# New planner costs, start slots and first-block slots for a recurrence woven into an MoE kernel

## The chip, the cores and the metric

The kernel runs on one core of one Trainium2 chip. The metric is the device time of one execution in microseconds (us); for the kernel before it is the median of three runs. Beside these there is one profiled execution with its trace. The engines are TensorE (PE in the profile, with its weight loads as PEld), VectorE (DVE), ScalarE (ACT), GpSimd (POOL) and SyncE (SP, which here only issues DMAs).

## The reference

The input `x` is 4 x 1024 tokens of 128 channels. Three layers change it in turn, each behind a layer norm:

```python
x = x + 0.5 * ffn(layernorm(x))
x = x + mamba(layernorm(x))
x = x + 0.5 * ffn(layernorm(x))

# ffn: 8 experts, all of them for every token, hidden width 512
h = silu(x @ w_gate[e]) * (x @ w_up[e]);  out += cw[:, e] * (h @ w_down[e])
# cw: product of two softmaxes over the experts, normalised

# mamba: 256 inner channels, 16 states, convolution over 4 steps
xs, z = split(x @ W_in);  xc = silu(conv4(xs) + conv_b)
dt = softplus((xc @ W_x)[:64] @ W_dt + b_dt);  B, C = the rest of xc @ W_x
h[t] = exp(dt*A) * h[t-1] + dt*xc*B[t]          # for each of 16 states n
y = sum_n h*C + xc*D;  out = (y * silu(z)) @ W_out
```

The recurrence over `t` runs along each of the four sequences.

## The kernel before, in words

The 4096 tokens are cut into 8 blocks of 512 (two blocks to a sequence). There are 16 passes of the ffn, one for each block before the recurrence, `(1, k)`, and one after it, `(2, k)`, in the order (1,0) (1,1) (1,2) (1,3) (2,0) (1,4) (2,1) (1,5) (2,2) (1,6) (1,7) (2,3) ... (2,7). A pass has 8 experts, an expert two **halves**. A half is one product for the gate (`pg`, six matmuls), one for the up branch (`pu`, six matmuls), the SiLU of the gate on ScalarE (`h`, L625), the multiply of both on VectorE (`h`, L657), and the products with the down weights into `pd` (L722; for the experts in `SPL` the operands are split in two parts on ScalarE and VectorE, `hh` L665 and `hl` L667, and go through L697 and L705). `pg` and `pu` have one buffer each: TensorE can't begin the next `pg` before the SiLU of the last has read it, nor the next `pu` before the multiply has read it. A half is counted as four **slots**, and the whole is 256 halves.

Into this stream the mamba layer of each block is woven. Its front (layer norm, `xs` and `z` products, four convolution taps, `xc`, `dbl`, `dt`, softplus, `dx`) is a list of events with a slot each; `START[k]` is the slot of block k that all are counted from, and `FRONT`/`REST` hold the slots of the single steps (`ta`, `xs`, `cv`, `ap`, `xp`, `dp`, `sp`, `df`, `n0`). Then come 16 states n in pairs. A pair is a burst on ScalarE: a table load, four `da` exponentials (L1002), a table load back for the SiLU. Each state then has four steps on VectorE: `prod` (`hb`, L1015), two scans (`hb`, L1021), and `read` (`da`, L1033; in the first block of a sequence also the copy of the last state, L1032). GpSimd adds the result to `y` (L1036). `bcb`, the broadcast of B and C, is loaded by SyncE into three buffers, the next one when a `read` has been issued. The end of a block (`gate`, `outproj`) waits for all 16.

The order on each engine is laid down when the program is built. A planner (`Plan`) keeps one clock for each engine in us, adds a cost for each step that it places, and takes VectorE's steps from two queues: `hi` for short steps (taps, splits, weightings) and `lo` for the recurrence. Before each multiply, `plan.now` fills VectorE with queued steps that would begin earlier than `SL` = 0.3 us before the multiply is ready. So a step's cost decides how many steps are put ahead of the next multiply. The costs in `LOCK` mark the steps that, like GpSimd's, read two operands from SBUF: the planner puts them outside of GpSimd's own steps. An event can have a readiness test: it is held back until the test is met by the planner's TensorE clock, but for no more than `WAIT` (12) slots, after which it is issued and waits on the chip.

ScalarE's bursts are gated by slots as well: `quiet` (softplus) and `turn` (exponentials) let one through only at every eighth slot, and never two in the same slot.

Of the kernel before, what the change touches and what calls it, by code (L numbers as in the profile page):

```python
# [18 lines left out]
BIG = 11  # L19
TMP = 3  # L20
TOL = 0.4
START = (72, 144, 232, 328, 432, 544, 656, 744)
REST = (4, 9, 17, 19, 23, 25, 29, 35, 37)
FRONT = {0: (5, 7, 8, 15, 16, 18, 21, 27, 29)}
ZT = {0: 11}
SOON = (0, 4, 6, 14, 15)
CALM = (4, 5)
# [16 lines left out]
FENDS = {0: 8, 1: 9, 9: 9, 15: 8}  # L44
OUT = 3
SL = 0.3
LOCK = (1.21, 0.71, 1.18, 0.66)
CAP = 5.8
NEVER = 1e9
WAIT = 12  # L50
# [3 lines left out]
class Plan:  # L54
# [74 lines left out]
    def run(self, it):  # L129
# [3 lines left out]
        self.dve = max(self.dve, it[2])  # L133
        if it[1] in LOCK:
            self.dve = self.unlocked(self.dve)
# [5 lines left out]
    def due(self, it):  # L141
        t = max(it[2], self.dve)
        return self.unlocked(t) if it[1] in LOCK else t

# [28 lines left out]
def tile_macaron_mamba_moe(  # L173
# [29 lines left out]
    NBLK = NB * L // TB  # L203
    BPB = L // TB
    FC = F // 128
    ND = DI // 128
# [11 lines left out]
    plan = Plan()  # L218

    def big(name):  # L220
        return sb.tile([P, 2, TB], F32, tag="big", bufs=BIG, name=name)
# [220 lines left out]
    silu_at, h_at = {}, {}  # L442
# [149 lines left out]
    def split(s, e):  # L592
        return s * E + e in SPL
# [34 lines left out]
    def half_products(s, c, i, tag, nm):  # L628
        d = ffn[s]
        e, f = divmod(c, FC)  # L630
        o = ps.tile([P, 2, TB], F32, tag=tag, bufs=1, name=f"{tag}_{nm}")
        cols = [slice((f + q) * P, (f + q + 1) * P) for q in range(2)]
        if (s, c, i) == (0, 0, 0):
            for q in range(2):
                T.matmul(o[:, q, :], wh[e][:, i, cols[q]], d["xh"], start=True, stop=False)
                T.matmul(o[:, q, :], wl[e][:, i, cols[q]], d["xh"], start=False, stop=False)
            for q in range(2):
                T.matmul(o[:, q, :], wh[e][:, i, cols[q]], d["xl"], start=False, stop=True)
            return o
        for q in range(2):  # L640
            T.matmul(o[:, q, :], wh[e][:, i, cols[q]], d["xh"], start=True, stop=False)  # L641
            T.matmul(o[:, q, :], wh[e][:, i, cols[q]], d["xl"], start=False, stop=False)  # L642
            T.matmul(o[:, q, :], wl[e][:, i, cols[q]], d["xh"], start=False, stop=True)  # L643
        return o

    def up_part(s, c):
        d = ffn[s]
        kind, k = order[s]
        e, f = divmod(c, FC)
        nm = f"{kind}_{k}_{c}"  # L650
        g = s * GPS * FC + c
        h = d["hp"]
        pu = half_products(s, c, 1, "pu", nm)
        t = max(silu_at[g], plan.on_pe(1.38, h_at.get(g - 2, 0.0)))

        def mul():
            V.tensor_tensor(h, h, pu, ALU.mult)  # L657

        h_at[g] = d["h_at", c] = d["h_at", c + 1] = plan.now(mul, 1.17, t, SL)
        if split(s, e):  # L660
            hh = sb.tile([P, 2, TB], F32R, tag="big", bufs=BIG, name=f"hh_{nm}")
            hl = sb.tile([P, 2, TB], F32R, tag="big", bufs=BIG, name=f"hl_{nm}")

            def high():
                S.copy(hh, h)  # L665
                d["hl", c] = d["hl", c + 1] = plan.put(
                    lambda: V.tensor_tensor(hl, h, hh.bitcast(F32), ALU.subtract), 1.18, plan.act + 0.1  # L667
                )

            d["hh", c] = d["hh", c + 1] = plan.act_put(high, 1.0, h_at[g], True)  # L670
            d["h", c] = d["h", c + 1] = hh, hl
        else:
            d["h", c] = (h[:, 0, :],)
            d["h", c + 1] = (h[:, 1, :],)
# [151 lines left out]
    riders, slot, burst_at, want = [], [0], [-1], set()  # L826
# [25 lines left out]
    def pool_need(it):  # L852
        if it not in pend:
            plan.need(lambda: it[3])
        while not it[3]:
            pool_one(None)
        return it[4]


    def mamba_events(k):  # L860
        d = {}
# [53 lines left out]
        def conv(i):  # L915
            if i == 0:
                d["cv"] = big(f"cv_{nm}")
            cv, xs = d["cv"], d["xs"]
            assert d["xsp"] > i
            def first_tap():  # L920
                S.activation(
                    cv[:, i, :], xs[:, i, 0:TB], AF.Identity,
                    bias=cb_sb[:, i : i + 1], scale=cw_sb[:, i, 0:1],
                )
                plan.put(lambda: tap(1), 0.71, plan.act + 0.61)

            it = plan.act_put(first_tap, 0.61, 0.0)
            d.setdefault("cv_it", []).append(it)

            def tap(q):  # L930
                V.scalar_tensor_tensor(
                    cv[:, i, :], xs[:, i, q : q + TB], cw_sb[:, i, q : q + 1], cv[:, i, :],
                    ALU.mult, ALU.add,
                )
                if q < 3:
                    plan.put(lambda: tap(q + 1), 0.71)
                else:
                    d["conv"] = d.get("conv", 0) + 1
                    d["cv_at"] = plan.dve + 0.1
# [58 lines left out]
        def exps(n):  # L998
            plan.need_lo(4 * OUT)
            da = d["da", n] = big(f"da_{nm}_{n}")  # L1000
            for i in range(ND):
                S.activation(da[:, i, :], d["dt"][:, i, :], AF.Exp, scale=A_sb[:, i, n : n + 1])  # L1002
            t = plan.on_act(1.22, 0.0, "exp")
            if n == 0:
                if fast:
                    plan.need(lambda: d["dx_it"][3])
                else:
                    t = max(t, pool_need(d["dx_it"]))
            for f, cost in ((prod, 1.21), (lambda n: step(n, 0), 1.2), (lambda n: step(n, 1), 1.2), (read, 1.2)):
                plan.put(lambda f=f: f(n), cost, t, low=True)  # L1010

        def prod(n):
# [5 lines left out]
        def step(n, i):  # L1018
            hb = d["hb"]
            da = d["da", n]  # L1020
            V.tensor_tensor_scan(  # L1021
                hb[:, i, :], da[:, i, :], hb[:, i, :],
                0.0 if first else st_sb[:, i, n : n + 1], ALU.mult, ALU.add,
            )
# [64 lines left out]
        fast = k == 0  # L1089
# [5 lines left out]
        zt = ZT.get(k, 14)  # L1095
        ta, xs, cv, ap, xp, dp, sp, df, n0 = FRONT.get(k, REST)

        def quiet():
            if d.get("dtp") != ND or slot[0] % 8 != 5:
                return False  # L1100
            want.add(k)
            return burst_at[0] < slot[0]
# [5 lines left out]
            (xs, inproj),  # L1108
            (xs, lambda: xsproj(0), lambda: max(free(), d["xlow"][4] if d["xlow"][3] else NEVER)),
            (cv, lambda: conv(0)),  # L1110
            (xs + 2, lambda: xsproj(1), free),
            (cv + 2, lambda: conv(1)),
            (zt, lambda: zproj(0), free),
            (zt + 2, lambda: zproj(1), free),
            (ap + w, act, lambda: d["cv_at"] if d.get("conv") == ND else NEVER),
            (xp + w, xproj, lambda: max(free(), d["xc_at"])),
            (dp + w, lambda: dtproj(0), lambda: max(free(), d["low"][4] if d["low"][3] else NEVER)),
            (dp + w + 2, lambda: dtproj(1), free),
            (sp + w, softplus, lambda: 0.0 if quiet() else NEVER),
            (df + w, dtfin),  # L1120
        ]
        mid = []

        def turn():
            fits = "dx_it" in d and slot[0] % 8 == 5 and burst_at[0] < slot[0]
            return 0.0 if fits and not want and len(plan.lo) <= QUEUE else NEVER

        for q in range(NS // 2):
            def two(q=q):
                burst_at[0] = slot[0]  # L1130
                while riders:
                    riders.pop(0)()
                exps(2 * q)
                exps(2 * q + 1)

            mid += [(n0 + 8 * int(SPR * q) + w, two, turn)]
        back = [
            (EPI + v + GT, gate, lambda: 0.0 if "scanned" in d else NEVER),
            (EPI + v + PO + (0 if quick else POW), outproj, lambda: max(free(), gated_at())),
        ]  # L1140

        def gated_at():
            return (d["gated"][4] if d["gated"][3] else NEVER) if "gated" in d else NEVER
# [5 lines left out]
    def add(base, evs, wait=WAIT):  # L1149
        chains.append([(max(0, base + ev[0]), wait, *ev[1:]) for ev in evs])  # L1150
# [15 lines left out]
    for s in range(len(order)):  # L1166
        add(8 * GPS * s, ffn_events(s))
        kind, k = order[s]
# [4 lines left out]
    for k in range(NBLK):  # L1173
        front, mid, back = mamba_events(k)
        add(START[k], front)
        add(START[k], mid, 99)
        add(START[k], back, 24 if k == NBLK - 1 else WAIT)
    for e in range(1, E):
        add(8 * (e - 1), [(WL, lambda e=e: load_expert(e)), (WS, lambda e=e: split_expert(e))])
    add(8 * E, [(-24, load_mamba)])  # L1180
# [5 lines left out]
    with tc.manual_schedule(engines={ET.PE, ET.Activation, ET.DVE, ET.Pool, ET.SP}):  # L1186
        half = 0
        while chains or done < nst:
            c = 2 * half
# [50 lines left out]
```

## Time and profile before

| | |
|---|---|
| median of three runs (lowest, highest) | 1266.12 us (1266.01, 1266.13) |
| the profiled execution's own time | 1265.99 us |
| its span, first to last instruction | 1264.2 us |
| DVE, ACT, POOL busy | 1138.2, 921.8, 706.1 us |
| granted TensorE clock | 1.0 |
| bytes read from HBM | 109.71 MB, 90 GB/s with the writes |

The profile gives busy time by engine, groups of equal instructions with their mean duration, and for each group the idle time of its engine just before, with what ended it. A record of a matmul lasts longer than the time to the next one, because matmuls are pipelined: in the trace a 128x512 matmul of the gate product lasts 0.40 us and the next one starts 0.23 us later. VectorE's and ScalarE's records overlap a little in the same way.

### The profile page before, as it was taken

The page shows a single profiled execution, that of the slowest core. Times are in us where ns is not written, and L with a number is a line of the kernel's source. Part 1 is how long each engine was busy: PE and PEld are TensorE (multiplying, and loading weights), DVE is VectorE, ACT ScalarE, POOL GpSimd, SP SyncE. Part 2 cuts the span into 40 slices and gives each one's busy share as a digit, 9 for nine tenths or more (in the row PEclk, how much of TensorE's full clock was granted, in tenths as well). Part 3 has the DMA queues.
Part 4 walks back from the last instruction along what each step waited for, and adds up shares of the span by engine and source line. Part 5 has one row for each costly group of instructions (what it writes and reads, how often), then busy time and mean ns, then how long its engine had stood idle before and what let it go on. Part 6 is the DMA issues. An engine that isn't in the chain of part 4 may idle for free.

```text
span 1264.2 us, 14417 instructions
## 1 busy us (share of the span) xinstructions
PE 1245.2 (99%) x4800; PEld 862.0 (68%) x4800; DVE 1138.2 (90%) x1286; ACT 921.8 (73%) x1326; POOL 706.1 (56%) x557
## 2 busy tenths in 40 slices
PE   9999999999999999999999999999999999999998
PEld 7776666666666666666666666666666666668787
DVE  6985699999899999999999999999999999998676
ACT  7684887776777768787788778778777776666653
POOL 1022465757568647775676567757775676554400
PEclk9999999999999999999999999999999999999999
DMA  4501333343343433334343353432433433311011
GB/s 147 158 26 34 107 112 86 101 112 82 81 107 97 118 91 95 93 99 110 99 100 96 92 119 84 120 98 82 113 98 79 110 92 109 103 56 42 26 43 25
DMA packets 75386, 115.09 MB, mean 91 GB/s; under 512 B 7472, under 2 KB 23728, under 8 KB 75312
## 3 DMA queue, kind: packets, MB, share of 16 engines
q1 hardware_dynamic: 75312, 114.19, 33.6%
q8 instruction: 37, 0.61, 0.2%
q14 instruction: 37, 0.30, 0.1%
HBM read 109.71 MB, written 4.46 MB: 90 GB/s over the span
## 4 chain that ended last, share of the span: by engine, by line
PE 70%; DVE 16%; ACT 5%; issue 5%; POOL 3%; DMA 1%; SPq 0%; DVEq 0%; ACTq 0%; POOLq 0%
PE pd L722 19%; PE pu L641 7%; PE pg L641 7%; PE pg L643 7%; PE pu L643 7%; PE pu L642 7%; PE pg L642 7%; DVE hb_m L1021 5%; DVE h L657 4%; PE pd L697 3%; DVE hb_m L1015 2%; DVE da_m L1033 2%; PE pd L705 1%; ACT da_m L1002 1%; ACT h L625 1%
## 5 line engine op out<-in xcount | busy, mean ns | idle before, releaser
L722 PE MATMUL pd<-h,wd 128*128 128x512 f32 x824 | 391.6, 592 | 1.2 <-ACT tmp L735 1.2
L657 DVE TENSOR_TENSOR h<-h,pu 128x1024 f32<-128x1024 f32 x256 | 311.1, 1215 | 76.9 <-PE pu L643 52.5
L1036 POOL TENSOR_TENSOR y_m<-y_m,da_m 128x1024 f32<-128x1024 f32 x128 | 310.5, 2426 | 106.5 <-DVE hb_m L1015 103.2
L625 ACT ACTIVATE h<-pg 128x1024 f32<-128x1024 f32 x256 | 262.7, 1026 | 140.2 <-PE pg L643 135.2
L641 PE MATMUL pg<-xh_f,wh 128*128 128x512 f32 x510 | 266.9, 523 | 0.7 <-ACT h L625 0.7
L744 POOL TENSOR_TENSOR tmp<-tmp,cwb 128x512 f32<-128x512 f32 x98 | 129.1, 1318 | 196.6 <-issue 106.2
L722 PEld LDWEIGHTS pd<-h,wd 128*128 128x128 f32 x824 | 153.5, 188 | 107.9 <-issue 89.6
L641 PE MATMUL pu<-xh_f,wh 128*128 128x512 f32 x512 | 205.8, 402 | 5.8 <-DVE h L657 5.6
L643 PE MATMUL pg<-xh_f,wl 128*128 128x512 f32 x510 | 201.1, 394 | 0.8 <-DVE wl L299 0.8
L643 PE MATMUL pu<-xh_f,wl 128*128 128x512 f32 x512 | 200.5, 392 | 0.0
L642 PE MATMUL pu<-xl_f,wh 128*128 128x512 f32 x512 | 199.9, 391 | 0.0
L642 PE MATMUL pg<-xl_f,wh 128*128 128x512 f32 x510 | 199.4, 391 | 0.0
L1015 DVE TENSOR_TENSOR hb_m<-dx_m,bcb_m 128x1024 f32<-128x1024 f32 x128 | 166.4, 1300 | 1.8
L1021 DVE TENSOR_TENSOR_SCAN hb_m<-da_m,st_sb,hb_m 128x512 f32<-128x512 f32 x128 | 164.2, 1283 | 2.3
L1002 ACT ACTIVATE da_m<-dt_m,A_sb 128x512 f32<-128x512 f32 x256 | 164.0, 711 | 0.6
L1021 DVE TENSOR_TENSOR_SCAN hb_m<-da_m,hb_m 128x512 f32<-128x512 f32 x128 | 156.7, 1224 | 2.6
L1033 DVE TENSOR_TENSOR da_m<-hb_m,bcb_m 128x1024 f32<-128x1024 f32 x128 | 155.8, 1217 | 1.5
L641 PEld LDWEIGHTS pg<-xh_f,wh 128*128 128x128 f32 x510 | 96.0, 188 | 64.8 <-issue 27.4
L747 POOL TENSOR_TENSOR acc<-acc,tmp 128x512 f32<-128x512 f32 x98 | 130.3, 1330 | 7.6
L642 PEld LDWEIGHTS pg<-xl_f,wh 128*128 128x128 f32 x510 | 96.3, 189 | 50.6 <-issue 36.5
L641 PEld LDWEIGHTS pu<-xh_f,wh 128*128 128x128 f32 x512 | 96.1, 188 | 35.4 <-DVE h L657 15.8
L643 PEld LDWEIGHTS pg<-xh_f,wl 128*128 128x128 f32 x510 | 95.6, 187 | 23.2 <-DVE wl L299 1.2
(181 smaller groups left out, 1494.7 us busy)
## 6 DMA issues: line engine op xcount, KB each, us to landing
bcb_m<-bc_m SPq DMA_DIRECT2D x128, 512.0 KB
cwb<-cd_f SPq DMA_DIRECT2D x128, 256.0 KB
out_dram<-x SPq DMA_DIRECT2D x13, 256.0 KB
x<-in_L_attn_x_dram SPq DMA_DIRECT2D x8, 256.0 KB
wraw<-in_L_ffn_w_gate_dram SPq DMA_DIRECT2D x8, 256.0 KB
wraw<-in_L_ffn_w_up_dram SPq DMA_DIRECT2D x8, 256.0 KB
wd<-in_L_ffn_w_down_dram SPq DMA_DIRECT2D x8, 256.0 KB
cd_f<-ct_f SPq DMA_DIRECT2D x64, 4.0 KB
```

Source lines behind the costliest of these rows:

```text
L625: S.activation(h, pg, AF.Silu)
L641: T.matmul(o[:, q, :], wh[e][:, i, cols[q]], d["xh"], start=True, stop=False)
L642: T.matmul(o[:, q, :], wh[e][:, i, cols[q]], d["xl"], start=False, stop=False)
L643: T.matmul(o[:, q, :], wl[e][:, i, cols[q]], d["xh"], start=False, stop=True)
L657: V.tensor_tensor(h, h, pu, ALU.mult)
L722: T.matmul(d["pd"], wd[e][:, cols], h[0], start=(f == 0), stop=(f == FC - 1))
L747: it = put(lambda: G_.tensor_tensor(acc, acc, t, ALU.add), 1.25, at)
L1002: S.activation(da[:, i, :], d["dt"][:, i, :], AF.Exp, scale=A_sb[:, i, n : n + 1])
L1015: mul = V.tensor_tensor(hb, d["dx"], bcb[:, 0:1, :].to_broadcast([P, ND, TB]), ALU.mult)
L1021: V.tensor_tensor_scan(hb[:, i, :], da[:, i, :], hb[:, i, :], 0.0 if first else st_sb[:, i, n : n + 1], ALU.mult, ALU.add,)
L1033: V.tensor_tensor(da, hb, bcb[:, 1:2, :].to_broadcast([P, ND, TB]), ALU.mult)
L1036: it = pool_put(lambda: G.tensor_tensor(d["y"], d["y"], da, ALU.add), 2.4, plan.dve)
```

## The change

No instruction is added or taken away: on each engine both programs hold the same instructions, in another order. The costs that the planner books for the multiply, the taps, `prod` and the first scan are set to other values (and `LOCK` with them, which finds a step by its cost; the weight split of an expert, 1.21, is no longer one of them). Blocks 5, 6 and 7 start 8, 16 and 24 slots sooner. Block 0's front has other slots, its first tap on ScalarE is issued at once instead of being queued, and its softplus and first exponentials may go at every fourth slot. The end of a block may be held back for 40 slots instead of 12 (24 for the last).

```diff
-START = (72, 144, 232, 328, 432, 544, 656, 744)
+START = (72, 144, 232, 328, 432, 536, 640, 720)
 REST = (4, 9, 17, 19, 23, 25, 29, 35, 37)
-FRONT = {0: (5, 7, 8, 15, 16, 18, 21, 27, 29)}
+FRONT = {0: (4, 6, 7, 11, 12, 14, 16, 19, 19)}
...
-LOCK = (1.21, 0.71, 1.18, 0.66)
+LOCK = (1.27, 0.75, 1.18, 0.66)
...
-        h_at[g] = d["h_at", c] = d["h_at", c + 1] = plan.now(mul, 1.17, t, SL)
+        h_at[g] = d["h_at", c] = d["h_at", c + 1] = plan.now(mul, 1.14, t, SL)
...
-                plan.put(lambda: tap(1), 0.71, plan.act + 0.61)
+                plan.put(lambda: tap(1), 0.75, plan.act + 0.61)
 
             it = plan.act_put(first_tap, 0.61, 0.0)
+            if fast:
+                plan.act_run(it)
...
-                    plan.put(lambda: tap(q + 1), 0.71)
+                    plan.put(lambda: tap(q + 1), 0.75)
...
-            for f, cost in ((prod, 1.21), (lambda n: step(n, 0), 1.2), (lambda n: step(n, 1), 1.2), (read, 1.2)):
+            for f, cost in ((prod, 1.27), (lambda n: step(n, 0), 1.25), (lambda n: step(n, 1), 1.2), (read, 1.2)):
...
-            if d.get("dtp") != ND or slot[0] % 8 != 5:
+            if d.get("dtp") != ND or slot[0] % (4 if fast else 8) != (1 if fast else 5):
...
             fits = "dx_it" in d and slot[0] % 8 == 5 and burst_at[0] < slot[0]
+            if fast and ("da", 0) not in d and "dx_it" in d and slot[0] % 4 == 1:
+                fits = True
...
-        add(START[k], back, 24 if k == NBLK - 1 else WAIT)
+        add(START[k], back, 40)
```

`fast` is true for block 0 alone.

## The prediction

> **What bounds the kernel now.** The page comes first: busy time by engine, then the groups (these lines are from the page).
>
> ```profile
> span 1264.2 us, 14417 instructions
> PE 1245.2 (99%) x4800; PEld 862.0 (68%) x4800; DVE 1138.2 (90%) x1286; ACT 921.8 (73%) x1326; POOL 706.1 (56%) x557
> ...
> L657 DVE TENSOR_TENSOR h<-h,pu 128x1024 f32<-128x1024 f32 x256 | 311.1, 1215 | 76.9 <-PE pu L643 52.5
> ...
> L1015 DVE TENSOR_TENSOR hb_m<-dx_m,bcb_m 128x1024 f32<-128x1024 f32 x128 | 166.4, 1300 | 1.8
> ```
>
> TensorE is busy 99% of the span, and the change takes no matmul away. What can be won is only the time in which TensorE waits. So the next view is who TensorE waits for (us in total, times, longest):
>
> ```profile
> PE pu L641 <- DVE h L657: 5.6, 11, 0.9
> PE pd L705 <- DVE hl L667: 1.7, 1, 1.7
> PE pd L722 <- ACT tmp L735: 1.2, 1, 1.2
> ...
> PE lt_f L485 <- DVE xl_f L471: 0.8, 2, 0.6
> PE pg L643 <- DVE wl L299: 0.8, 1, 0.8
> PE pg L641 <- ACT h L625: 0.7, 1, 0.7
> ```
>
> All fifteen rows of this view add up to 15.3 us, of which about 3 belong to the start and the last pass's end. A wait costs a little more than it shows: a matmul's record lasts 0.40 us and the next may start 0.23 after it, so TensorE is stopped 0.17 longer than it counts as idle. The eleven waits for the multiply thus cost 5.6 + 11 x 0.17 = 7.5 us. That is the largest part and the one that the planner's costs govern. The third view is the load by stage (busy us in 64 us: PE, PEld, DVE, ACT, POOL):
>
> ```profile
> 64.00:128.00 64.00, 61.66 (x255) 45.86 (x254) 43.31 (x57) 41.34 (x73) 13.63 (x20) 1.00 0.10 30
> 1024.00:1088.00 64.00, 63.19 (x242) 42.58 (x241) 62.69 (x63) 43.14 (x56) 45.72 (x33) 1.00 0.39 108
> ```
>
> Before the recurrence VectorE has 20 us of 64 to spare, in the middle 1.3. A step too many ahead of a multiply isn't made up for quickly there. The last view is VectorE's timeline around one such wait:
>
> ```profile
> 235.71 1.22 DVE L657 TENSOR_TENSOR h<-h,pu 128x1024 f32<-128x1024 f32 x1 [0.42 <-PE pu L643]
> ...
> 241.91 1.21 DVE L657 TENSOR_TENSOR h<-h,pu 128x1024 f32<-128x1024 f32 x1
> 243.03 1.23 DVE L1015 TENSOR_TENSOR hb_m<-dx_m,bcb_m 128x1024 f32<-128x1024 f32 x1
> 244.29 2.49 DVE L1021 TENSOR_TENSOR_SCAN hb_m<-da_m,hb_m 128x512 f32<-128x512 f32 x2
> ...
> 248.03 1.21 DVE L657 TENSOR_TENSOR h<-h,pu 128x1024 f32<-128x1024 f32 x1
> ```
>
> The multiply takes 1.12 from start to next start (241.91 to 243.03), `prod` before a scan 1.26, the scan pair 2.53 to the copy. From the multiply at 235.71 to the end of the one at 248.03 VectorE needs 13.53 us. TensorE's steps from the end of the `pu` that the first reads to the start of the `pu` that waits for the third are three `pg` (1.37 each), two `pu` (1.37), six down products (0.856), four `v` (0.229) and a transpose: 13.03. The overrun is 0.50; the trace shows a wait of 0.36, which with the 0.17 is 0.53. So static sums of this kind predict the waits.
>
> **The change, part by part.** The sum is made against the profiled execution's 1265.99 us; the median, 1266.12, is 0.13 above. Both programs hold 4290, 1264, 1248, 562 and 389 instructions on PE, DVE, ACT, POOL and SP, ScalarE's with 154 changes of table in both. Only the order counts.
>
> *Planner costs.* A multiply booked at 1.14 is what the trace shows; `prod`, first scan and taps rise by 0.06, 0.05 and 0.04. A state is booked at 4.92 instead of 4.81, where the trace shows 1.26 + 2.53 + 0.08 + 1.13 = 5.00 above. Fewer steps go ahead of a multiply. I made the sum of the example for every multiply and up to 14 multiplies back, with the means of the groups: before, 19 places have an overrun above -0.25 us; after, 13. Added up from that threshold it is 5.06 us before and 3.14 after, 62%. At the example's place the changed order has the last `read` and copy behind the multiply: 12.08 against 13.03, no wait. Of the 7.5 us I take off 38%: **-2.9**. Bounds: nothing, and all of it, -7.5. What hides the rest is the room for a multiply, one down pair and one `pg` less itself (1.71 + 1.37 - 1.13 = 1.95 us); without that cover each state between two multiplies (1.13 + 5.00 against 4.46) would cost 1.67.
>
> *ScalarE's bursts.* The same sum for the SiLU (it must end before the next `pg`): before 2 places above -0.25, which add up to 0.62; after 5, adding up to 1.47. Three are new in kind. In block 0 softplus and the first exponentials now stand in neighbouring halves (overrun -0.03); in pass (1,2) a burst goes at once after `h` (0.02 and 0.09); in pass (1,7) block 5's last exponentials and block 6's softplus are neighbours: SiLU 0.92, load 1.29, two small and four large exponentials 2.7, load 1.29, SiLU 0.92, load 1.29, softplus 1.08, copy 0.49, load 1.29, SiLU 0.92, in all 12.2 against TensorE's 12.0. Before, one overrun of 0.22 became the 0.7 us wait (0.87 with the 0.17); by the same ratio 1.47 becomes 2.0: **+1.1**. Bounds: -0.9 (no such wait) and +3.5 (0.87 at all five places).
>
> The row for these loads: one at 145.42 lasts 1.28 and the SiLU behind it starts at 146.72, 0.02 us after it. [...]
>
> *Block 0's first tap at once.* On ScalarE it now stands between the copy of `xs0` and the copy `tmp` that frees `pd`, for which TensorE waits at 106.98. The row of the tap (L921) has 0.81 us, 0.71 to the next start. The down products, the `xs1` products and the next `pg` are queued behind that wait: **+0.7**. Below zero it can't go; at most 0.8.
>
> *Pass (1,0).* VectorE's order moves `hl` of the third half into a gap of 1.47 us ahead of the multiply at 24.61, and the `hl` that TensorE waits for at 34.17 comes one multiply (1.13) sooner. But from 34.64 to 70.55 VectorE runs with only 1.0 us of idle time, to the expert weight `wl` that TensorE waits for at 70.6. The same steps lie between in both orders, so most comes back there: **-0.4**, between -1.2 and +0.4.
>
> *Block 7 sooner.* The `xl` of the last pass is made two halves earlier, and its logits 1.5, so the wait of 0.6 (L485) at 1171.4 goes: **-0.7**. Next late is the transpose of the weights (L556, 0.5), where the order is as before.
>
> *What moves and costs nothing.* The recurrences of blocks 5 and 6 begin in the same halves as before (152, 176), block 7's two earlier (200 for 202): they start when the block before leaves the queue, not at `START`. Block 0's first `prod` comes 2 halves sooner, the last `read` of all 1.5. SyncE's queue issues block 0's B and C about one half sooner; the first `bcb` issue was at 129.49 and `prod` at 143.12, so 13.6 us shrink to about 9. DMA moved 0.76 MB from 129.4 to 135, more than one `bcb` of 0.5 MB, so it has landed by then. If that failed, `prod` would hold the next multiply and TensorE behind it, up to 2 us. GpSimd's order and load are the same, but its long steps (2.4 us) will meet VectorE elsewhere: `prod` was held to 2.74 us at worst, a tap to 2.86, so one new meeting costs up to 2.1 and one that goes saves as much. I take 0, by the equal number of steps.
>
> Sum: -2.9 + 1.1 + 0.7 - 0.4 - 0.7 = **-2.2**, 1265.99 to 1263.8, and the same against the median within 0.1. I predict 1263.8.
>
> **Rivals.** Bounds for "same" are 0.2%, 2.5 us: 1263.6 to 1268.7, about what a measurement of this kernel can tell from no change.
>
> *All of VectorE's lateness goes.* The two halves' lead of block 0 is kept, and the multiply is never late: -7.5, -0.7, with +0.7 for the tap: 1258.5. For it: 6 of the 11 waits lie at places where the changed order has no overrun above -0.25. Against: three places still overrun by 0.3 to 0.5, and ends of blocks are as full as before.
>
> *The change doesn't do what it says.* Since the late recurrences begin where they did, there is no more room in the middle; tight places only move. The tap and the bursts cost what the planner saves: 1266.0, within 0.5 either way.
>
> *Slower: neighbouring bursts on ScalarE.* In blocks 0 and 6 two bursts follow each other, and SiLU, multiply and `pg` all queue behind the second. If its real length is over the sum by 1.5 us at each of the five places, TensorE waits 7.5 us there instead of the 0.9 of before. The other terms add up to -3.3, so the total is +3.3: 1269.3. It is slower than before from 0.8 us a place, by more than can be doubted from 1.2. Against: nothing stands between a load and its user in the rows.
>
> **How the numbers follow.** Forecast (1262 to 1265.5) 0.45; all lateness gone, or near to it (below 1262) 0.20; nothing (1265.5 to 1268) 0.20; slower, beyond that, 0.15. Of the forecast half lies below 1263.6. Faster by over 0.2% is 0.20 + 0.23 = 0.43; slower than 1268.7 keeps 0.13; within, 0.44. The range leaves out a tenth on each side: 1258.0, just beyond the whole of the lateness, to 1268.9, just short of the ScalarE rival's time.
>
> **What would show it.** In the profile after: TensorE's waits for the multiply fall from 5.6 us to about 3.5 in seven or eight waits; the wait for SiLU rises from 0.7 to about 1.5; the wait for `tmp` near 107 rises from 1.2 to 1.9; `hl` falls to about 0.5 and `wl` rises by nearly as much; L485's 0.6 is gone; the matmul count and ScalarE's loads are the same. I am wrong if the multiply's waits don't fall, or if TensorE waits anywhere more than 3 us for GpSimd or a DMA.

## The result: 1274.19 us, 0.65% slower

| | before | after |
|---|---|---|
| median of 4 runs each (lowest to highest) | 1266.07 us (1265.76 to 1266.13) | 1274.19 us (1273.82 to 1275.47) |
| ratio, 95% interval | | 1.0065, 1.0051 to 1.0079 |
| profiled run: time, span | 1265.99, 1264.2 us | 1274.01, 1272.2 us |

The changed kernel is 8.1 us slower, against a forecast of 2.2 us faster and a range that ended at 1268.9. The page's first lines of the changed kernel:

```profile
span 1272.2 us, 14425 instructions
PE 1249.2 (98%) x4800; PEld 861.1 (68%) x4800; DVE 1136.6 (89%) x1286; ACT 922.1 (72%) x1326; POOL 705.8 (55%) x557
```

VectorE, ScalarE and GpSimd have the busy time of before. TensorE's rises by 4.0 of the 8 us, with the same number of matmuls; the other 4 us are idle time. TensorE's waits in the changed kernel (us in total, times, longest):

```profile
PE pd L705 <- DVE hl L667: 4.6, 3, 2.6
PE pd L722 <- ACT tmp L735: 2.0, 1, 2.0
PE pg L641 <- ACT h L625: 1.9, 4, 0.9
PE pg L643 <- DVE wl L299: 1.3, 2, 0.8
PE pu L641 <- DVE h L657: 1.2, 3, 0.5
PE pg L641 <- DVE wh L298: 1.1, 1, 1.1
...
PE xs_m L890 <- DVE ex_f L506: 1.0, 1, 1.0
```

The wait that the change is about, the multiply (`pu` <- `h`), fell from 5.6 us in 11 waits to 1.2 in 3, further than forecast. But the operand splits, `hl`, `wl` and `wh`, went from 2.5 to 7.0 us, and `tmp`, SiLU and `xs_m` grew by 3. To see where, I took for each half how much later its `pu` starts than in the kernel before. I call this its lag: +0.3 us at half 12, +3.3 at 16, +2.9 at 20, +6.5 at 28, +7.5 at 60, +6.2 at 224, +9.0 at 228, +8.0 at the end. (Half 24, at +7.6, has six more matmuls of the front ahead of it than before, some 1.4 us of work that is only moved; at the halves listed the number is equal.) So three places lose, pass (1,0), block 0's front and halves 224 to 228, and a middle gains.

**Pass (1,0).** VectorE's rows there, changed kernel (start, length, engine, line):

```profile
68.85 1.21 DVE L657 TENSOR_TENSOR h<-h,pu 128x1024 f32<-128x1024 f32 x1
69.98 0.68 DVE L298 CAST wh<-wraw 128x1024 fp32r<-128x1024 f32 x1
70.70 1.23 DVE L299 TENSOR_TENSOR wl<-wraw,wh 128x1024 fp32r<-128x1024 f32 x1
...
74.65 1.22 DVE L657 TENSOR_TENSOR h<-h,pu 128x1024 f32<-128x1024 f32 x1 [2.12 <-PE pu L643]
75.78 1.22 DVE L667 TENSOR_TENSOR hl<-h,hh 128x1024 fp32r<-128x1024 f32 x1
```

And the same place in the kernel before:

```profile
67.60 0.69 DVE L298 CAST wh<-wraw 128x1024 fp32r<-128x1024 f32 x1
68.20 1.21 DVE L657 TENSOR_TENSOR h<-h,pu 128x1024 f32<-128x1024 f32 x1
69.33 1.22 DVE L299 TENSOR_TENSOR wl<-wraw,wh 128x1024 fp32r<-128x1024 f32 x1
...
71.13 1.21 DVE L667 TENSOR_TENSOR hl<-h,hh 128x1024 fp32r<-128x1024 f32 x1
73.30 1.22 DVE L657 TENSOR_TENSOR h<-h,pu 128x1024 f32<-128x1024 f32 x1 [0.95 <-PE pu L643]
```

There the casting of this expert weight (`wh`) stood one multiply sooner, ahead of the multiply at 68.20, and `hl` stood ahead of the next multiply. Now TensorE waits 1.25 us for it at 70.81 and 0.63 for `wl` at 71.98. So its next `pu` is late as well, VectorE idles 2.12 us for it, and the `hl` that could have filled this gap stands behind the multiply: TensorE waits another 1.76 us at 77.06. (The times at a place, here and below, are taken from issue to issue; they are some 0.17 us longer than in the view of the waits.)

**Block 0's front.** On ScalarE the first tap stands ahead of the copy `tmp` that TensorE waits for:

```profile
109.45 0.81 ACT L921 ACTIVATE cv_m<-xs_m,cb_sb,cw_sb 128x512 f32<-128x512 f32 x1
110.17 0.56 ACT L735 COPY tmp<-pd 128x512 f32<-128x512 f32 x1
```

Stretches of 2, 4 and 4 us around this wait and behind it (stretch, length; busy time of PE, PEld, DVE, ACT, POOL; granted clock; DMA):

```profile
110.00:112.00 2.00, 1.21 (x3) 0.73 (x4) 0.75 (x1) 0.74 (x2) 1.18 (x1) 0.94 0.00 0
112.00:116.00 4.00, 4.00 (x10) 2.45 (x10) 1.26 (x2) 1.40 (x2) 1.64 (x3) 0.61 0.31 66
116.00:120.00 4.00, 4.00 (x18) 2.73 (x16) 1.47 (x3) 2.11 (x3) 0.00 (x0) 1.00 0.00 0
```

TensorE waits 2.2 us, up to 110.79, and from 111.75 its granted clock is 0.5 for 3.41 us: 10 matmuls in 4 us instead of 18.

**The end.** VectorE's rows there, changed kernel:

```profile
1137.35 1.22 DVE L1017 TENSOR_TENSOR hb_m<-dx_m,bcb_m 128x1024 f32<-128x1024 f32 x1
1138.61 2.61 DVE L1023 TENSOR_TENSOR_SCAN hb_m<-da_m,st_sb,hb_m 128x512 f32<-128x512 f32 x2
1141.13 1.21 DVE L657 TENSOR_TENSOR h<-h,pu 128x1024 f32<-128x1024 f32 x1
1142.25 1.21 DVE L667 TENSOR_TENSOR hl<-h,hh 128x1024 fp32r<-128x1024 f32 x1
```

The `hl` at 1142.25 stands behind `prod`, two scans and the multiply of a later half. TensorE waits 2.7 us for it, to 1143.52. In the kernel before, the same `hl`, here the first row, stood ahead of that multiply and of the recurrence's steps:

```profile
1131.23 1.21 DVE L667 TENSOR_TENSOR hl<-h,hh 128x1024 fp32r<-128x1024 f32 x1
...
1134.10 1.21 DVE L657 TENSOR_TENSOR h<-h,pu 128x1024 f32<-128x1024 f32 x1
1135.23 1.22 DVE L1015 TENSOR_TENSOR hb_m<-dx_m,bcb_m 128x1024 f32<-128x1024 f32 x1
```

### The profile page after: what moved, and what is told of

It reads as the page before. It is cut to its first block, busy times and chain, and to the rows that moved or that the text cites. A ratio compares the mean times of both kernels' runs of the same rounds, so it can differ in the third digit from the quotient of the medians.

```text
span 1272.2 us, 14425 instructions
## 1 busy us (share of the span) xinstructions
PE 1249.2 (98%) x4800; PEld 861.1 (68%) x4800; DVE 1136.6 (89%) x1286; ACT 922.1 (72%) x1326; POOL 705.8 (55%) x557
## 4 chain that ended last, share of the span: by engine, by line
PE 80%; DVE 9%; ACT 4%; issue 3%; POOL 2%; DMA 1%; SPq 0%; DVEq 0%; ACTq 0%; POOLq 0%
PE pd L722 22%; PE pu L641 8%; PE pg L641 8%; PE pu L643 8%; PE pg L643 8%; PE pu L642 8%; PE pg L642 8%; DVE h L657 3%; PE pd L697 3%; DVE hb_m L1023 2%; PE pd L705 1%; DVE da_m L1035 1%; DVE hb_m L1017 1%; PE po_m L1075 1%; ACT da_m L1004 1%
```

## The experiments

**Theory A:** single places where VectorE's order puts a split behind other work (pass (1,0), the end), and block 0's front, each with its own price. **Rival B:** block 0's front, with its bursts on ScalarE, is the whole loss. **Rival C:** the new booked costs overfill VectorE wherever they are used. (The expectations call them shorter; only the multiply's is.) Times are medians with the lowest and highest run; a ratio is to the kernel before, run again in the same round (medians 1266.01, 1266.17 and 1266.12), with its 95% interval.

The order in pass (1,0) has its cause in one line of the diff. `LOCK` holds costs, and the planner asks `if it[1] in LOCK` (L134, L143): a cost is a key. The split of an expert weight (`wl`, L299) is booked at 1.21 and stood under the key of `prod`. The change moves `prod` and the key to 1.27, and L299 stays at 1.21: it stops being a step that is kept apart from GpSimd's. The section on the change says so; the prediction gives it no price.

**1. The key put back** (e1_lock_121), in the changed kernel:

```diff
-LOCK = (1.27, 0.75, 1.18, 0.66)
+LOCK = (1.27, 0.75, 1.18, 0.66, 1.21)
```

> The kernel after, with 1.21 put back into LOCK, so that the planner treats the split of an expert's weights as it did before; nothing else. Theory A (three places, of which pass (1,0) is one: its order of wh, wl and hl costs 3.3 us by half 16): 1270.9, and TensorE's waits for wh, wl and hl before 78 us fall from 5.1 to about 2.5 us. Rival B (the loss is in block 0's crowded front and the neighbouring bursts on ScalarE): 1274.2 as before, since the front stays. Rival C (the new costs put too many steps ahead of the multiply everywhere): 1274.2 within 1, the early order being a small part.

Measured: 1269.84 us (1268.09 to 1272.75), ratio to before 1.0027 (1.0016 to 1.0037). The wait for `wh` is gone, `wl` is back at one wait. One entry of a tuple is worth 4.3 us, in the place that A said and more than its 3.3; B and C can't have it.

**2. The tap queued again** (e2_tap_queued), in the changed kernel:

```diff
-            if fast:
-                plan.act_run(it)
```

> The kernel after, with block 0's first tap queued on ScalarE again instead of issued at once; all else stays, the crowded slots of block 0 too. Theory A (at 110.8 us TensorE waits 2.2 us for tmp behind that tap, and then gets half of its clock for 3.4 us): the wait falls to 1.3, the clock stays at 1.0, 1274.2 - 0.9 - 1.75 = 1271.5. If only the wait counts and the clock drops all the same: 1273.3. Rival B (front crowded as a whole): 1274.2 or above, since the taps then come later in the same few slots. Rival C: 1274.2.

Measured: 1279.92 (1276.81 to 1279.99), 1.0106 (1.0089 to 1.0123). A miss: slower instead of faster. Three of the four runs are at 1279.9 with a mean clock of 0.996, the profiled one at 1276.81 with 0.999. `tmp` fell to 1.2 us as expected, but with the front's fewer slots a later tap makes `xc` late, and `dbl_m` waits 2.7 us near 127. The tap at once is not a burden on the new front; it is what the fewer slots need.

**3. The wait filled** (e3_filled_wait): eight matmuls whose result is not used, put ahead of the products that wait for `tmp` near 110.

```diff
+        if (s, e, f) == (1, 2, 0):
+            fill = ps.tile([P, ND, TB], F32, tag="hb", bufs=1, name="fill")
+            for q in range(8):
+                T.matmul(fill[:, 0, :], wh[e][:, 0, 0:P], d["xh"], start=True, stop=True)
```

> The kernel after, with eight matmuls (128x512, 0.23 us each, results unused) put on TensorE into the 2.2 us wait for tmp at 110.8 us; all waits stay. Theory A's part on the clock (the wait itself takes the clock to one half for 3.4 us, which costs 1.75 us): the clock stays at 1.0 and the time is 1272.4; the wait itself, 2.2 us, is still there as work. Without the effect of the clock: 1274.2, or up to 0.3 above, if the eight overrun the wait. If the drop has another cause than the wait: 1274.2 with the drop still at 111.7.

Measured: 1274.60 (1273.82 to 1275.38), 1.0064 (1.0049 to 1.0079): no gain in the median. In the trace the half clock behind 111.75 is gone, and halves 20 to 24 cost 3.0 us where they cost 4.7: 1.6 us for the clock at that place, near the 1.75 expected. But in this profiled run the clock is halved at 72.69 and 1144.48 instead, beside the waits in pass (1,0) and at the end. In this trace filling one wait didn't save the clock, with the others left.

**4. Block 0's front as before** (e4_front_undone): `FRONT[0]`, the tap, `quiet` and `turn` of the kernel before, the rest changed.

```diff
-FRONT = {0: (4, 6, 7, 11, 12, 14, 16, 19, 19)}
+FRONT = {0: (5, 7, 8, 15, 16, 18, 21, 27, 29)}
```

> The kernel after, with the whole front of block 0 as before (FRONT, the tap queued, softplus and exponentials at every eighth slot); costs, START and the held-back end stay. Theory A: pass (1,0) and the end as in the kernel after (+3.3, +3.1), no long wait at 110, the middle 1.8 better: 1266.1 + 4.6 = 1270.7. Rival B: all of the loss is gone, 1264 to 1266. Rival C: 1273 to 1274, since the costs stay.

Measured: 1271.11 (1271.03 to 1271.30), 1.0037 (1.0024 to 1.0050). The lag at half 60 is 2.6 us instead of 7.5, and the end still loses 4.3 us. In the changed kernel it loses 2.9; here the clock is halved from 1138.86, beside the wait for `hl`, which makes the other 1.4. So the front cost 3.1 us here and not everything: B falls, as the whole of it.

**5. The end's booking undone** (e5_back_undone):

```diff
-        add(START[k], back, 40)
+        add(START[k], back, 24 if k == NBLK - 1 else WAIT)
```

> The changed kernel with the mixing of a finished block booked 12 slots (24 for block 7) after its start as before, instead of 40. VectorE's order then differs only behind h_2_5_28. Theory A (single places where VectorE's order puts a split or a multiply behind other work and TensorE waits for it): the order sets hl_2_6_2 in front of h_2_6_6 again, so the 2.72 us that TensorE waits at 1143.52 for hl goes. But laying VectorE's durations end to end, the multiply h_2_6_8 is then 2.7 us late where it was not late at all, so TensorE gets a wait for h of 2 to 2.7 us in its place: 1273 to 1274.5, and the wait of 40 by itself is worth nothing. Rival B (block 0's faster front is the whole loss): 1274, with no new wait for h. Rival that the end is simply undone by this number: 1271.3.

Measured: 1278.61 (1277.36 to 1280.63), 1.0092 (1.0077 to 1.0107). A miss for the number, which A put at 1273 to 1274.5. The exchange came as A said, but at a worse rate: `hl` still waits 1.4 us at 1141.93, the multiply 2.9 at 1147.25, and the last products (`po_m`) 1.9 at 1151.5. VectorE's rows in this kernel:

```profile
1143.53 1.28 DVE L1023 TENSOR_TENSOR_SCAN hb_m<-da_m,st_sb,hb_m 128x512 f32<-128x512 f32 x1
1144.84 1.22 DVE L1035 TENSOR_TENSOR da_m<-hb_m,bcb_m 128x1024 f32<-128x1024 f32 x1
1145.99 1.21 DVE L657 TENSOR_TENSOR h<-h,pu 128x1024 f32<-128x1024 f32 x1
```

A scan and a `read` stand ahead of the multiply here; in the changed kernel two scans stood ahead of the split. So the wait of 40 slots was no mistake by itself: without it the rest is slower.

**6. Only the sooner starts** (e6_start_alone), in the kernel before:

```diff
-START = (72, 144, 232, 328, 432, 544, 656, 744)
+START = (72, 144, 232, 328, 432, 536, 640, 720)
```

> The kernel before with only the sooner starts of blocks 5, 6 and 7 (536, 640, 720), all booked durations, block 0's front and the waits as before. Theory A: VectorE's order changes only from the seventh stretch of passes on; laid end to end, its lateness rises from 2.6 us to 10.5 us, all of the rise in passes (1,7) and (2,3) (h_1_7_26 1.7, h_1_7_30 2.0, h_2_3_0 .9, h_2_3_6 1.1, h_2_3_10 1.4), because the booked 1.17 for a multiply and 1.21 for a product leave fewer free slots and the sooner block takes them at once. Some of these follow one another and share one delay, so 4 to 8 us slower: 1270 to 1274, with the waits of TensorE for h and SiLU there. Rival B (all the loss is block 0's front): 1266.0. Rival C (shorter booked costs overfill VectorE everywhere): 1266.0 as well, since the costs are those of before.

Measured: 1270.72 (1269.29 to 1271.04), 1.0027 (1.0017 to 1.0037). The number is A's, the mechanism is not. The multiply's waits fell, from 5.6 to 3.6 us; what was lost between halves 160 and 180, 5.2 us, is mostly one wait of 3.1 us of `v_m` for ScalarE (3.3 with the 0.17) and the clock, halved from 868.09 behind it. ScalarE's rows in this kernel:

```profile
863.50 1.28 ACT L518 ACT_TABLE_LOAD   x1
...
865.05 2.54 ACT L1002 ACTIVATE da_m<-dt_m,A_sb 128x512 f32<-128x512 f32 x4
867.50 0.67 ACT L979 ACTIVATE dt_m<-v_m,bdt_sb 128x512 f32<-128x512 f32 x1
```

The `dt_m` that frees `v_m` stands behind a whole burst. By themselves the sooner starts set a burst in front of block 6's softplus path. Beside the new costs, the key and the 40 slots (item 11 has the same starts) this wait is not there; which of the three takes it away was not taken apart.

**7. Only the tap** (e7_tap_alone), in the kernel before:

```diff
             it = plan.act_put(first_tap, 0.61, 0.0)
+            if fast:
+                plan.act_run(it)
```

> The kernel before with only block 0's first tap issued at once on ScalarE instead of waiting in the queue of steps. Theory A: TensorE's wait for tmp near 107 us grows from 1.2 to about 2.0 us, as in the changed kernel, and nothing else moves: +0.9, 1266.9; with the clock at half for 3.4 us behind the wait, as in the changed kernel's profiled run, up to 1268.6. Rival B (block 0's front is the whole loss, and the tap its main part): +4 us or more, 1270. Prediction on record for this part: +0.7.

Measured: 1267.55 (1265.95 to 1267.82), 1.0003 (0.9993 to 1.0012). The wait for `tmp` grew from 1.3 to 2.2 us at 107.69 as forecast. But the wait of 0.87 for SiLU at 147.8 went, so four of the ten runs are at 1265.95 to 1266.23 with a mean granted clock of 1.000: there the tap costs nothing. The other six are at 1267.45 to 1267.82 with 0.998 or 0.999; in the profiled one the clock is halved from 107.69 for 3.41 us. If the tap has a price, it is the chance of that, 1.6 us. The kernel before has 9 of its 23 runs of this round at 1267.5 and above too, so these runs don't show that the tap raises the chance.

**8. Combined** (e8_combined): the changed durations and the sooner late blocks, the key kept, block 0's front as before, block 6 and the mixing moved a little.

```diff
-START = (72, 144, 232, 328, 432, 536, 640, 720)
+START = (72, 144, 232, 328, 432, 536, 648, 720)
-LOCK = (1.27, 0.75, 1.18, 0.66)
+LOCK = (1.27, 0.75, 1.18, 0.66, 1.21)
-        add(START[k], back, 40)
+        add(START[k], back, 36)
```

> The changed kernel's durations (multiply 1.14, product 1.27, first scan step 1.25, tap 0.75) and sooner late blocks, with 1.21 kept in LOCK so that the splits of expert weights stay locked steps, block 0's front as before, block 6 at 648 instead of 640 and 36 instead of 40 slots before the mixing. Theory A, from VectorE's durations laid end to end: no split later than in the kernel before (1.88 us in sum), multiplies and SiLU 2.3 us late in sum against 2.6 before (5.1 against 6.7 if every one has 0.25 us less room), so 0.3 to 1.8 us faster than before: 1264.2 to 1265.7, say 1264.9. Rival C (shorter booked costs overfill VectorE wherever they are used): 1269 or more, since the costs are those of the changed kernel. Rival B (front alone): 1266.

Measured: 1264.27 (1264.11 to 1265.75), 0.9980 (0.9970 to 0.9990): faster than both. C falls, since all the changed costs are in it. Its waits:

```profile
PE pd L705 <- DVE hl L667: 1.6, 1, 1.6
PE po_m L1073 <- DVE zs_m L1057: 1.6, 1, 1.6
PE pu L641 <- DVE h L657: 1.3, 4, 0.5
PE pg L641 <- ACT h L625: 1.2, 2, 0.7
PE pd L722 <- ACT tmp L735: 1.2, 1, 1.2
```

The multiply's gain is kept (1.3 us), the splits are back at one wait each; a new one of 1.6 us for the gated output (`zs_m`) takes part of it.

The next four put one part of the change back into this kernel at a time.

**9. Without the key** (e9_best_no_lock):

```diff
-LOCK = (1.27, 0.75, 1.18, 0.66, 1.21)
+LOCK = (1.27, 0.75, 1.18, 0.66)
```

> The combined kernel of the last round with 1.21 taken out of LOCK again, as in the changed kernel, and nothing else: VectorE's order of pass (1,0) becomes the changed kernel's. Theory A: the waits for wl at 61.6, wh at 70.8, wl at 72.0 and hl at 77.1 come back, together 4.6 us, and hl at 34 and wl at 70.6 get shorter; by the lags of the runs so far (2.9 at half 20 in the changed kernel, -.85 in the combined one) 3.8 slower than the combined kernel: 1268.0, with one dip of the clock 1269.7. Rival: the key in LOCK matters little and pass (1,0) lost by other parts of the change: 1264.3.

Measured: 1268.96 (1267.78 to 1270.90), 1.0020 (1.0010 to 1.0029): 4.7 us over the combined kernel's median, 3.7 from lowest to lowest; the rest is the clock (four runs with 0.997 or 0.998 are at 1269.4 to 1270.9; in the profiled run it is halved from 72.71, just behind the waits for `wh` and `wl`).

**10. With the changed front** (e10_best_front): item 4's diff turned round, with the tap and the bursts.

> The combined kernel with block 0's whole front of the changed kernel (first tap at once, fewer slots, bursts every 4 slots). Theory A: the wait for tmp near 110 grows to 2.2, xs_m near 217 waits 1.2 behind a burst of ScalarE, SiLU is late by .5 to 1.1 at 144, 177 and 239; by the lags of the run with 1.21 back in LOCK (.9 at half 20, 4.0 at half 60) some 3 us slower than the combined kernel: 1267.5, with a dip of the clock behind the wait for tmp 1269.2. The sums of VectorE's durations alone give 1.66 against 2.32, so 0.7 faster, 1263.6: that is the rival, that the front is harmless and the loss is in the splits alone.

Measured: 1267.51 (1267.18 to 1269.06), 1.0011 (1.0002 to 1.0020): +3.2. The waits that grew are `tmp` by 0.9, `xs_m` near 213 by 1.2, and SiLU near 140, 173 and 235 by 1.2 together (one of 0.5 near 354 went). So the rival, that the front is harmless and all of the loss is in the splits, is wrong.

**11. With the changed end** (e11_best_end): block 6 at 640, 40 slots before the mixing.

```diff
-START = (72, 144, 232, 328, 432, 536, 648, 720)
+START = (72, 144, 232, 328, 432, 536, 640, 720)
```

> The combined kernel with block 6 at 640 and 40 slots before the mixing, as in the changed kernel. Theory A: hl_2_6_2 stands behind h_2_6_6 and two products again, and TensorE waits 2.7 us for it near 1138; by the lags 2.9 slower between halves 224 and 228, less what the combined kernel itself loses at halves 228 to 232 (1.8, a wait for zs): +1 to +2.9, 1265.3 to 1267.2, with a dip of the clock behind the wait 1268.8. Rival: the slots of the late blocks are free (0): 1264.3.

Measured: 1266.73 (1265.85 to 1268.95), 1.0001 (0.9992 to 1.0010): +2.5, from lowest to lowest +1.7. `hl` is back at two waits, the longer 2.6 us, and the wait for `zs_m` is gone.

**12. Only the front's fewer slots** (e12_best_slots): `FRONT[0]` as changed; tap queued, bursts eight slots apart.

```diff
-FRONT = {0: (5, 7, 8, 15, 16, 18, 21, 27, 29)}
+FRONT = {0: (4, 6, 7, 11, 12, 14, 16, 19, 19)}
```

> The combined kernel with only the fewer slots of block 0's front (4, 6, 7, 11, 12, 14, 16, 19, 19); the first tap stays queued, ScalarE's bursts stay 8 slots apart. It tells apart what of the front costs. Theory A (the crowded bursts of ScalarE are what costs): the waits for SiLU and xs_m stay away, at most 1 us: 1264.0 to 1265.3. Rival (the slots themselves push the front's products in front of the splits and multiplies): the whole 3 us, 1267.3. In the changed kernel with the tap queued TensorE waited 2.7 us for xc_m near 127; if that is of the slots and not of the bursts, it shows here too, 1267.

Measured: 1271.39 (1269.69 to 1273.06), 1.0032 (1.0021 to 1.0044): +7.1, more than the whole front. The wait of item 2 is there:

```profile
PE dbl_m L954 <- ACT ls_f L490: 2.7, 1, 2.7
```

And ScalarE's rows there:

```profile
123.20 1.06 ACT L948 ACTIVATE xc_m<-cv_m 128x1024 f32<-128x1024 f32 x1 [3.81 <-DVE cv_m L931]
124.16 0.56 ACT L490 COPY ls_f<-lt_f 16x512 f32<-16x512 f32 x1
```

On ScalarE `ls_f`, which frees the bank that `dbl_m` writes, stands behind `xc`, its operand, and `xc` began only after 3.81 us without work for want of the convolution's taps on VectorE. `dbl_m` comes four slots sooner now, and neither of the two does. So the rival's reading is right here, and A's is not: the bursts are not what costs most, the slots are, and the tap at once together with the closer bursts gives about half of it back (7.1 to 3.2 by the medians, 5.6 to 3.1 by the lowest runs).

## Why the prediction was wrong

The step that failed is the sum of what TensorE waits for. It was made for the multiply and the SiLU alone, and pass (1,0), where the change puts splits of operands behind other work, was let through at -0.4 without one; put back by itself, the key that makes this order costs 4.7 us. Both signs of being wrong that the prediction names stayed away: the multiply's waits fell, and no wait for GpSimd or a DMA is near 3 us.

The parts, put back one at a time, account for the result. From the medians: combined kernel against before -1.9, key +4.7, front +3.2, end +2.5, in all +8.5; measured +8.1. From the lowest runs the parts give +6.7; the changed kernel's own lowest run, at +8.1, has a mean clock of 0.998, so some of the clock's loss, 1.6 us a time, is in it.

- **Multiply's waits, -2.9.** Right in its direction. As a wait it was half of what came: with 0.17 for each, as the prediction counts, 7.5 us became 1.7, so -5.8. As time it was twice what came: between halves 60 and 224, where nine of the eleven waits lay, the changed kernel gains 1.4 us. Other waits come up there, such as `pt_m` of block 5 with 0.9 and 0.3 us.
- **Pass (1,0), -0.4: this is the step that failed.** I saw that the order changes there and let it pass with "the same steps lie between in both orders". I laid VectorE's durations end to end only for the multiply and the SiLU, and not for the three splits, each of which TensorE also waits for. In the traces the waits for `hl`, `wh` and `wl` are 2.5 us before and 7.0 in the changed kernel. With the splits in the sum, item 8's order was forecast at 1264.9 and measured at 1264.27. What came back as I had said is the gain itself: the wait at 34.17 shrank, and by half 12 that was used up. What I had not seen are the three waits behind it. Their cause, a constant that is also a key, I had named ahead of the prediction, and not asked what it does to the order. Measured: the changed kernel is 2.9 us behind at half 20, where the combined one is 0.9 ahead, so 3.8, and 4.7 in item 9.
- **Block 7 sooner, -0.7.** Right: the wait of 0.6 at L485 is gone, the lag falls by 0.8 between halves 232 and 236, and next late is the transpose (L556, 0.5), as said. What has no term is the `hl` at 1143.52 with 2.7 us, which the late blocks' slots bring about a few halves sooner. It is the same omission, a split. It does not come from block 7's start as such, which is the same in item 8, where this wait is absent; item 11 brings it back with block 6 at 640 and 40 slots.
- **The tap, +0.7.** The wait grew by 0.9, a little over the bound of 0.8. By itself it cost nothing in the runs with a full clock (item 7), since the wait for SiLU at 147.8 went, and what I had no term for is the clock behind it.
- **ScalarE's bursts, +1.1.** SiLU's waits rose from 0.7 to 1.9 us, with 0.17 for each by 1.7: right, and somewhat small. The rival at 1269.3 was right in sign for a wrong reason: no wait for SiLU is longer than 0.9 us. (By its own sum it passes the bound of 2.5 us from 1.3 us a place, not from 1.2.)
- **What the front does to `xs_m` and `dbl_m`.** The prediction has no term for it. Moved events were costed by the engines' sums, not by whether each operand is there at its new slot: `xs_m` waits 1.2 us for a bank that the router's `ex_f` frees, behind a multiply.

The order of steps by itself does not tell in which run the clock is halved (the last section has what the traces show of it), so by an estimate from the 1.6 us of items 3 and 7 the medians of kernels with waits of 2 us and more are uncertain by one or two times that. It also stays open what the new costs alone, without the sooner starts, are worth.

## What to carry to other kernels

When an engine's order is laid down anew, make the list of everything that the bound engine waits for, and lay the durations end to end for each entry of it, not only for the wait that the change is meant to remove. Before changing a number in a planner, look for every place where that number is compared: here a cost was also a key, and one entry left out lost more (4.7 us) than the combined kernel gained (1.9). Several parts of such a change hold each other up (fewer slots lose more without the sooner tap, the sooner starts lose by themselves), so undoing one of them is no measure of its price; adding one to a good kernel is nearer to it.

## What the runs showed of the hardware

The granted clock of TensorE falls to 0.5 for 3.413 us beside waits that are shorter than that. In the changed kernel it followed 2.2 us of waiting; in item 9 it followed two waits of 1.3 and 0.6 us near 71 and 72, with matmuls between them. The traces' records of the clock change only whole multiples of 3.41333 us apart: in the changed kernel the stretch at full clock ahead of the halved one lasts 105.813 us, 31 times that, and the one behind it 1157.118, 339 times; in the kernel before the only full stretch lasts 1256.105, 368 times; and the two halved stretches of item 3's trace begin 1071.785 us apart, which is 314 times. So in these traces the changes lie on a grid of this step. I call its steps windows. None of the windows ahead of the halved stretches named here was idle throughout: in the changed kernel TensorE is busy for 1.36 us of it, and the longest wait in the traces of items 3 and 9 is 2.6 us.

How much idle time stood in a window ahead of a halved stretch can be read by laying this grid over each trace, away from the kernel's first and last 4 us. In the kernel after (window; length, busy time of PE first):

```profile
108.33:111.75 3.42, 1.36 (x5) 0.49 (x3) 1.71 (x2) 1.87 (x3) 0.93 (x1) 1.00 0.00 0
1139.16:1142.57 3.41, 1.76 (x8) 1.13 (x6) 3.38 (x4) 0.83 (x2) 1.88 (x1) 1.00 0.01 2
1142.57:1145.98 3.41, 2.46 (x13) 2.07 (x14) 3.41 (x5) 1.43 (x2) 1.02 (x1) 1.00 0.00 0
```

The first holds the whole wait for `tmp`, 2.05 us of idle time, and a halved stretch follows. The longer wait for `hl` at the end is cut by the grid into 1.65 and 0.95, and none follows. In all fourteen traces each of the eight windows with 2.0 us or more of idle time is followed by a halved stretch, five with 1.56 to 1.79 are too, others with up to 1.86 are not, and none below 1.56 is. (Idle time is the profile's, whose matmul ends are modelled.)

Where the grid lies against the program differs between the traces: the full clock begins 6.855 us after the first instruction in the kernel before and 5.932 in the changed one. That it differs from run to run of the same program too, and with it whether a given wait is followed by a halved stretch, is my reading and was not shown, since one execution of each kernel was traced. In the last round 21 of the 28 runs of the kernel before are at 1265.8 to 1266.4 us with a mean clock of 0.999 or 1.000, and six at 1267.4 to 1267.7 with 0.998. The step of 1.5 us is near the price of one such stretch in items 3 and 7, 1.6, and it is most of the spread of this kernel's runs.
